# Moving the relation gathers of a graph-and-expert kernel: nine a step in its first pass, the rest behind the expert tiles of block 2

## The chip, the cores and the metric

The kernel runs on one core of a Trainium2 chip. A core has five engines that run their own instruction streams: TensorE (PE: matrix multiplications, with weight loads PEld), VectorE (DVE), ScalarE (ACT), GpSimd (POOL) and SyncE (SP, which here only issues transfers and loads registers). Transfers are made by 16 DMA engines; SP, ACT and POOL each feed them from a queue of their own. Every stream is in order: an instruction that waits holds all that follow it on the same engine. The metric is the device time of one execution in microseconds (us), lower is better.

## What is computed

The reference is a stack of four blocks, each added to its input, over 3125 nodes of 256 values with 103125 edges sorted by destination:

```
x = x + gnn(layernorm(x))         # block 1: 3 layers, mean over in-edges, two 256x256 products
x = x + moe16(layernorm(x))       # block 2: 16 experts, hidden 512, best 2 by gate; layernorm at the end
x = x + clifford(layernorm(x))    # block 3, below
x = x + moe8(layernorm(x))        # block 4: 8 experts, hidden 1024, best 2
```

Block 3 is where the relations come in:

```
h_src = h_hc[src]
r_uv  = r_hc[edge_type]                       # one of 500 relation rows per edge
m = clifford_linear(h_src * r_uv, msg_w, msg_b)
gate = sigmoid(r_uv @ gate_w.T + gate_b)
m = m * gate * norm                           # norm from the degrees of both ends
h_agg = segment_sum(m, dst)
h_out = clifford_linear(h_hc + h_agg, upd_w, upd_b)
```

For each edge the row of its relation has to be fetched from a table of 500 rows (256 values and the gate, 257 floats). The rows do not depend on the nodes, only on the edges' types, so they can be fetched long before block 3 needs them.

## The kernel before

**Blocks and slots.** The nodes lie in NB = 25 blocks of 128. Block 1's first pass over the blocks (L640 to L664, a loop of NB + 3 = 28 steps, software-pipelined over up to four blocks) sorts each destination block's edges into 26 tiles of 128 slots. A step loads a window of edges for block i (`load`, L512, `win`; each half has its place read into a register of SP), ranks them on VectorE (`rank`, L522 `kb`, L531 `member` from TensorE's `prior`, L533, L536), permutes and lays out block i-1 (`permute`, `lay`: TensorE's `ends`, ScalarE's `held` at L587, VectorE's `main_t`, the relation number of every slot), builds adjacency cells for block i-2 (`build`: `oh_end` on VectorE, `block` on TensorE, `cell` on ScalarE, stored by SP at L631) and finishes the first layer for block i-3 (`sums_of` with `z` on TensorE, `finish` on VectorE). Layers 2 and 3 follow as two passes that read the stored cells back; they are called layer 1 and layer 2 in the code, and nothing of them is edited.

**Relation groups.** There are 25 x 26 = 650 slot tiles. Their relation rows are gathered three tiles at a time, 217 groups. `fetch_relations(n, after)` issues the next n groups: VectorE writes the three columns of indices into `paced` (L296) by an operation that also reads `after`, and so it can run only when `after` is there; GpSimd gathers three times 128 rows (L300, an indirect DMA each) into a staging tile `rel_rows` (four buffers); and then `store_relations` has SP write the group before it to DRAM, `r_seq` (L311). Block 3 later reads the groups back in order (`rg_seq`, L1396). So `after` decides when a group is gathered at the earliest. A scheduler puts each engine's instructions in order when the kernel is built, by when their inputs should be there; a group whose `after` is early may so be placed far ahead of where the code has it.

Before the change the groups are fetched so: 95 in pass 1 (up to four a step: one paced by the rank's `qi` at L558, two by `moved` of blocks i-1 and i-2 at L649 and L652, one by `done`, what `finish` returns, at L664), 50 in each of the next two passes, 10 in block 2 after its routing has found the best experts (`top_v`), and the last 12 after block 2's tiles in the code, with `after=beta`. As `beta` is a small load made at the start of block 2, the scheduler puts the 12 ahead of the tiles too.

**Block 2.** `moe` (L922) routes the nodes: it finds the best two experts for each, gives each pair a place, and writes the token indices `tok_g` (L1065), the weights `wt_q` (L1075) and each tile's expert number. Then 34 tiles of 256 tokens run (`expert_tile`, L1119 to L1176): SP loads the expert number into a register and issues the loads of `w1_t` and `w2_t` (L1122, L1125, three buffers each); GpSimd gathers two `xt` of 128 rows two tiles ahead (L249); TensorE transposes them (`pt`, L1130), multiplies (`ph`, L1145), ScalarE and VectorE apply the ReLU (`hid`), TensorE multiplies again (`py`, L1163); VectorE scales (`y`, L1166, eight buffers), and GpSimd scatters with addition into `f_total` (L1168). The two scatters of a tile touch different rows and do not wait for one another, but the first of a tile waits until those of the tile before have landed. After each tile up to the 34th `moe` calls `beside(t)`, which here adds `beta` to one block of `xs`. A loop for further tiles follows (L1188), which does not run with these inputs; all engines meet at its test, and their transfers must have landed.

**Block 3.** Its preparation (L1216 to L1297) loads weights (`mw`, `uw`, L1237) and makes the kernels `km` and `ku`, reads `f_total` back, applies the layernorms, and writes for each of the 25 blocks a scaled copy `hs` (four buffers), split into `hc_part` for TensorE and stored by SP to `hc_rows` (L1285). Then the messages: for 650 main tiles TensorE selects the source rows (`hg_ps`, L1422) and VectorE multiplies with `rg_seq` (`prod`, L1425); 225 spill tiles gather source rows `hg` from `hc_rows` and relation rows `rg` with GpSimd (L249) instead.

**Room.** `paced` and the staging tiles live in pools of `rel_ctx` (L283 to L285), which is closed after block 2 (L1204). The pools that block 3 opens next take that room, and their tiles wait until its last readers and writers are done.

Of the kernel before, what the change touches and what calls it, by code (L numbers as in the profile page):

```python
# [37 lines left out]
F32 = mybir.dt.float32  # L38
BF = mybir.dt.bfloat16
F16 = mybir.dt.float16  # L40
I32 = mybir.dt.int32
# [7 lines left out]
P = 128  # L49
N = 3125  # L50
NB = 25
# [28 lines left out]
def gnn_moe_kernel(  # L80
# [166 lines left out]
    def gather(pool, table, width, ids, name, bufs):  # L247
        rows = pool.tile([P, width], F32, name=name, bufs=bufs)
        nc.gpsimd.indirect_dma_start(out=rows, out_offset=None, in_=table,  # L249
                                     in_offset=bass.IndirectOffsetOnAxis(ap=ids, axis=0))  # L250
        return rows
# [70 lines left out]
    with ExitStack() as block:  # L322
# [66 lines left out]
        with ExitStack() as first:  # L389
# [251 lines left out]
            for i in range(NB + 3):  # L641
                if i < NB:
                    loaded[i] = load(i)
                    ranked[i] = rank(i, loaded[i])
                if 0 <= i - 1 < NB:
                    moved[i - 1] = permute(i - 1, loaded.pop(i - 1), *ranked.pop(i - 1))
                    lay(i - 1, moved[i - 1])
                    if i > 1:
                        fetch_relations(1, words_of(moved[i - 1]))  # L649
                if 0 <= i - 2 < NB:  # L650
                    if i > 2:
                        fetch_relations(1, words_of(moved[i - 2]))  # L652
                    built[i - 2] = build(i - 2, moved.pop(i - 2))
                for b in range(i * SB, min((i + 1) * SB, NB)):
                    spread(b, 0, psum.tile([P, D + 1], F32, name="z", bufs=2)[:, :D],
                           psum.tile([P, 4, P], F32, name="block", bufs=2).rearrange(
                               "p a q -> p (a q)"))
                if i == 3:
                    nc.sync.dma_start(base, x)
                if 0 <= i - 3 < NB:  # L660
                    z = sums_of(i - 3, built.pop(i - 3), 0, psum)
                    done = finish(i - 3, z, 0)
                    if i > 3:
                        fetch_relations(1, done.bitcast(I32))  # L664

        with ExitStack() as flags:
            one = flags.enter_context(tc.tile_pool(name="g0_deg0", bufs=1))
# [252 lines left out]


    def moe(tag, n_exp, hidden, b1, w1, w2, b2, act, ln, x_rows, total, usual,  # L922
            beside=lambda t: None):

# [4 lines left out]
        with ExitStack() as block:  # L931
# [176 lines left out]
            with ExitStack() as run:  # L1108
# [10 lines left out]
                def expert_tile(t):  # L1119
                    e = nc.sync.value_load(exp_i[0:1, t:t + 1], min_val=0, max_val=n_exp - 1)  # L1120
                    w1_t = wpool.tile([P, 1, KD, hidden], F32, name="w1_t")
                    nc.sync.dma_start(w1_t, w1[bass.ds(e, 1), :, :].rearrange(  # L1122
                        "e (p k) f -> p e k f", k=KD))
                    w2_t = wpool.tile([P, 1, nj, D], F32, name="w2_t")
                    nc.sync.dma_start(w2_t, w2[bass.ds(e, 1), :, :].rearrange(  # L1125
                        "e (j p) d -> p e j d", p=P))
                    pt = psum.tile([P, KD, TS], F32, name="pt")
                    for half, xt in enumerate(ahead.pop(t)):
                        for k in range(KD):
                            nc.tensor.transpose(pt[:, k, half * P:(half + 1) * P],  # L1130
                                                xt[:, k:D:KD], ident)
                    xT = work.tile([P, KD, TS], F32, name="xT")
                    for k in range(KD):
                        if ln is None:
                            nc.vector.tensor_copy(xT[:, k, :], pt[:, k, :])  # L1135
                        else:
                            nc.vector.tensor_scalar(xT[:, k, :], pt[:, k, :],
                                                    ln_t[:, 0, k, t:t + 1], ln_t[:, 1, k, t:t + 1],
                                                    op0=ALU.mult, op1=ALU.add)
                    hid = work.tile([P, nj, TS], F32, name="hid")  # L1140
                    for j0 in range(0, nj, 2):
                        ph = psum.tile([P, 2, TS], F32, name="ph", bufs=3)
                        for j in range(j0, j0 + 2):
                            for k in range(KD):
                                nc.tensor.matmul(ph[:, j - j0, :],  # L1145
                                                 w1_t[:, 0, k, j * P:(j + 1) * P], xT[:, k, :],
                                                 start=k == 0, stop=k == KD - 1)
                        for j in range(j0, j0 + 2):
                            if act == AF.Relu and j % 2:
                                nc.vector.tensor_scalar(hid[:, j, :], ph[:, j - j0, :],  # L1150
                                                        b1_t[:, j, t:t + 1], 0.0,
                                                        op0=ALU.add, op1=ALU.max)
                            else:
                                nc.scalar.activation(hid[:, j, :], ph[:, j - j0, :], act,  # L1154
                                                     bias=b1_t[:, j, t:t + 1])
                    for half in range(TS // P):
                        q = t * (TS // P) + half
                        of = slice(half * P, (half + 1) * P)
                        py = psum.tile([P, D], F32, name="py")
                        nc.tensor.matmul(py, oh[:, t:t + 1].to_broadcast([3 * 32, P]), b2_sb,  # L1160
                                         start=True, stop=False)
                        for j in range(nj):
                            nc.tensor.matmul(py, hid[:, j, of], w2_t[:, 0, j, :], start=False,  # L1163
                                             stop=j == nj - 1)
                        y = work.tile([P, D], F32, name="y", bufs=8)
                        nc.vector.tensor_scalar(y, py, wt_q[:, q:q + 1], None, op0=ALU.mult)  # L1166

                        st = nc.gpsimd.indirect_dma_start(  # L1168
                            out=total, in_=y, in_offset=None,
                            out_offset=bass.IndirectOffsetOnAxis(ap=tok_s[:, q:q + 1], axis=0),  # L1170
                            compute_op=ALU.add)
                        if half:
                            tc.declare_no_dep(st.ins, group=f"{tag}_add{t}", reason="other rows")
                        tc.add_to_no_dep_group(f"{tag}_add{t}", st.ins)
                    if t < usual:
                        beside(t)  # L1176

                def run_tiles(first, end):
                    for t in range(first, min(first + 2, end)):
# [15 lines left out]
    with ExitStack() as block:  # L1195
        keep = block.enter_context(tc.tile_pool(name="f0_tokens", bufs=1))
        beta = keep.tile([P, D], F32, name="beta")
        nc.scalar.dma_start(beta, bcast(f0_beta, D))
        fetch_relations(10, top_v[:, NB - 1, :].bitcast(I32))
        moe("f0", 16, 512, f0_b1, f0_w1, f0_w2, f0_b2, AF.Relu, None, f0_x, f0_total, 34,  # L1200
            lambda t: t < NB and nc.vector.tensor_add(xs[:, t, :], xs[:, t, :], beta))
        fetch_relations(len(of_group), beta.bitcast(I32))
        store_relations()
    rel_ctx.close()  # L1204

# [4 lines left out]
    f1_x = dram.tile([NP, D], F32, name="f1_x")  # L1210
    f1_total = dram.tile([NP + TS, D], F32, name="f1_total")
    with ExitStack() as block:
        keep = block.enter_context(tc.tile_pool(name="g1_keep", bufs=1))
        h = keep.tile([P, NB, D], F32, name="hc")

# [104 lines left out]
        with ExitStack() as run:  # L1320
# [80 lines left out]
            def summands():  # L1401


                for b in range(NB):
# [5 lines left out]
                    for n, (_, spilled, t) in enumerate(order):  # L1410
                        ids = spill_d[:, b, :] if spilled else main_d[:, b, :]
                        if t % DG == 0:
                            d_oh[spilled] = drops(ids[:, t:min(t + DG, ids.shape[1])])
                        prod = work.tile([P, W], F32, name="prod", bufs=4)
                        if spilled:
                            hg = gather(work, h_rows, W, spill_s[:, b, t:t + 1], "hg", 6)
                            rg = gather(work, r_rows, W, spill_t[:, b, t:t + 1], "rg", 6)
                        else:
                            sh = t - (t > b)
                            hg = psum.tile([P, W], F32, name="hg_ps", bufs=3)  # L1420
                            for i in (2, 1, 0):
                                nc.tensor.matmul(hg, s_oh[:, t, :], part[:, sh, i, :W],  # L1422
                                                 start=i == 2, stop=i == 0)
                            rg = relation(b * NS + t)
# [76 lines left out]
```

## Time and profile before

| | |
|---|---|
| median of 3 runs | 3060.95 us (3058.07 to 3086.63) |
| profiled execution | 3058.8 us, span 3056.9 us, mean granted TensorE clock 0.914 |
| pass 1 | about 100 to 667 us |
| layers 1 and 2 | 667 to 1323 us |
| block 2: routing, tiles, loop exit | to 1396, 1428 to 1725, 1729.5 us |
| block 3: preparation, messages | 1730 to 1814, 1814 to 2546 us |
| block 4 | 2546 to 3057 us |
| busy over the span | PE 81%, DVE 57%, POOL 51%, ACT 14% |
| relation gathers | 650, 765 us of POOL, mean 1177 ns |

The stages are read off the first and last instructions of their lines. The profile comes from one execution and gives for every group of instructions its line, engine, operation, tiles, count, busy time, mean duration, and what ended the idle time before it; "<-issue" means that nothing the profile shows was waited for. PEclk is the clock that TensorE was granted, as a share of full speed.

### The profile page before, as it was taken

Reading aid. Unit: us, or ns where it says so; the run is one execution under the profiler, and the core shown is the slowest. Engines: PE = TensorE matmul, PEld = TensorE weight load, DVE = VectorE, ACT = ScalarE, POOL = GpSimd, SP = SyncE. Lnnn points to the kernel's source line nnn. Section 1 sums busy time; section 2 is a strip of 40 time slices with the busy share of each in tenths; the row PEclk is TensorE's granted clock in tenths of the full one; section 3 lists DMA queues with packets and bytes.
Section 4 is the critical chain, followed back from the end, with each engine's and each line's share of the span. In section 5 each row is a group of like instructions: output and inputs, shape, how many; then the busy total and the mean of one; then the engine's idle time right before and its main releaser. Section 6 shows DMA issues by size and latency. Waiting matters only on the chain. (4 is left out here: it accounts for less than half of the span.)

```text
span 3056.9 us, 47874 instructions
## 1 busy us (share of the span) xinstructions
PE 2490.5 (81%) x17712; PEld 1978.3 (65%) x17712; DVE 1754.0 (57%) x4664; ACT 432.4 (14%) x1119; POOL 1568.3 (51%) x1383
## 2 busy tenths in 40 slices
PE   1877667769878999943999419999999996899997
PEld 0565556645667588832888306777777775788886
DVE  6978777856555466651333377888788887111110
ACT  1311211213000300000111050000000000222221
POOL 1176876761455166675566326666666660333331
PEclk9988888879989999966999759999999997899998
DMA  5156665663667278865888447777777771766663
GB/s 181 38 176 183 178 188 169 180 211 98 214 199 233 94 253 277 258 183 162 223 200 200 95 148 247 252 248 247 244 245 245 250 217 31 225 181 180 180 176 94
DMA packets 294159, 581.10 MB, mean 190 GB/s; under 512 B 77947, under 2 KB 176956, under 8 KB 289940
## 3 DMA queue, kind: packets, MB, share of 16 engines
q1 hardware_dynamic: 204243, 386.35, 37.2%
q0 software_dynamic: 76992, 177.86, 23.4%
q10 hardware_dynamic: 12672, 13.65, 1.5%
q8 instruction: 145, 2.38, 0.3%
q14 instruction: 107, 0.87, 0.1%
HBM read 433.05 MB, written 151.13 MB: 191 GB/s over the span
## 5 line engine op out<-in xcount | busy, mean ns | idle before, releaser
L300 POOL DMA_INDIRECT rel_rows<-r_rows,paced x650 | 765.1, 1177 | 657.4 <-issue 158.2
L363 PE MATMUL z<-part_hi,cell 128*128 128x256 bf16 x3750 | 685.7, 284 | 27.2 <-issue 26.2
L360 PE MATMUL z<-part_lo,cell 128*128 128x256 bf16 (+1 forms) x1875 | 531.8, 284 | 23.9 <-issue 19.2
L1434 PE MATMUL ps<-prod,d_oh 128*128 128x257 f32 x1750 | 519.7, 391 | 28.9 <-issue 15.1
L363 PEld LDWEIGHTS <-cell 128*128 128x128 bf16 x3750 | 373.3, 101 | 96.7 <-issue 43.4
L1422 PE MATMUL hg_ps<-hc_part,s_oh 128*128 128x257 bf16 x1950 | 328.4, 275 | 106.4 <-DMA hg<-hc_rows,spill_s 106.4
L1168 POOL DMA_INDIRECT f_total<-y,tok_s x126 | 198.3, 1574 | 351.9 <-DVE y L1166 277.0
L249 POOL DMA_INDIRECT hg<-hc_rows,spill_s x225 | 234.0, 1040 | 266.3 <-DVE prod L1425 128.6
L1163 PE MATMUL py<-w_t,hid 128*128 128x256 f32 x1472 | 335.1, 382 | 8.6 <-ACT hid L1154 8.6
L1145 PE MATMUL ph<-xT,w_t 128*128 128x256 f32 x1472 | 335.5, 385 | 0.8
L1425 DVE TENSOR_TENSOR prod<-hg_ps,rg_seq 128x257 f32<-128x257 f32 x650 | 270.0, 421 | 103.9 <-PE hg_ps L1422 67.9
L1434 PEld LDWEIGHTS ps<-prod,d_oh 128*128 128x128 f32 x1750 | 276.1, 191 | 81.1 <-issue 31.3
L1422 PEld LDWEIGHTS <-s_oh 128*128 128x128 bf16 x1950 | 191.5, 99 | 204.0 <-DVE s_oh L1378 106.8
L1166 DVE TENSOR_SCALAR y<-py,wt_q 128x256 f32<-128x256 f32 x126 | 60.9, 484 | 444.9 <-PE py L1163 433.4
L1163 PEld LDWEIGHTS py<-w_t,hid 128*128 128x128 f32 x1472 | 273.9, 191 | 55.8 <-ACT hid L1154 9.0
L1145 PEld LDWEIGHTS ph<-xT,w_t 128*128 128x128 f32 x1472 | 279.8, 192 | 43.7 <-DVE xT L1135 3.1
L249 POOL DMA_INDIRECT rg<-r_rows,spill_t x225 | 234.3, 1041 | 68.6 <-issue 68.6
L360 PEld LDWEIGHTS <-cell 128*128 128x128 bf16 x1875 | 191.7, 102 | 54.8 <-issue 24.7
L1154 ACT ACTIVATE hid<-ph,b_t 128x256 f32<-128x256 f32 x300 | 129.4, 471 | 650.0 <-PE ph L1145 621.8
L249 POOL DMA_INDIRECT xt<-f_x,tok_g x126 | 123.5, 980 | 94.1 <-DVE wt_q L1075 38.3
L501 DVE TENSOR_TENSOR oh_end<-held,iota 128x1024 bf16<-128x1024 f16 (+3 forms) x150 | 150.2, 1016 | 0.2
L862 DVE TENSOR_REDUCE some_src<-cell 128x25 f32<-128x3200 bf16 x25 | 87.2, 3487 | 93.8 <-DMA cell<-cells 79.5
(307 smaller groups left out, 2821.9 us busy)
## 6 DMA issues: line engine op xcount, KB each, us to landing
r_seq<-rel_rows SPq DMA_DIRECT2D x216, 385.5 KB
rg_seq<-r_seq SPq DMA_DIRECT2D x216, 385.5 KB
w_t<-in_L_ffn_W_dram SPq DMA_DIRECT2D x58, 1024.0 KB
cell<-cells SPq DMA_DIRECT2D x50, 800.0 KB
w_t<-in_L_ffn_w_dram SPq DMA_DIRECT2D x68, 512.0 KB
s_row<-main_s SPq DMA_DIRECT2D x25, 832.0 KB
cells<-cell SPq DMA_DIRECT2D x25, 800.0 KB
rel_rows<-r_rows,paced POOLq DMA_INDIRECT x650
```

Source lines behind the costliest of these rows:

```text
L249: nc.gpsimd.indirect_dma_start(out=rows, out_offset=None, in_=table, in_offset=bass.IndirectOffsetOnAxis(ap=ids, axis=0))
L300: nc.gpsimd.indirect_dma_start(out=rows[:, j, :], out_offset=None, in_=r_rows, in_offset=bass.IndirectOffsetOnAxis(ap=types[:, j:j + 1], a ...
L360: nc.tensor.matmul(z[:, :width], cell[:, sh, :], part_lo[:, sh, :width], start=sh == 0, stop=False)
L363: nc.tensor.matmul(z[:, :D], cell[:, sh, :], part_hi[:, sh, i, :], start=False, stop=sh == NB - 1 and i == 1)
L501: nc.vector.tensor_tensor(oh[:, :n, :, :], ids[:, :, None, :].to_broadcast([P, n, width, 2]), table[:, None, :width, :].to_broadcast([P, n ...
L1145: nc.tensor.matmul(ph[:, j - j0, :], w1_t[:, 0, k, j * P:(j + 1) * P], xT[:, k, :], start=k == 0, stop=k == KD - 1)
L1154: nc.scalar.activation(hid[:, j, :], ph[:, j - j0, :], act, bias=b1_t[:, j, t:t + 1])
L1163: nc.tensor.matmul(py, hid[:, j, of], w2_t[:, 0, j, :], start=False, stop=j == nj - 1)
L1168: st = nc.gpsimd.indirect_dma_start(out=total, in_=y, in_offset=None, out_offset=bass.IndirectOffsetOnAxis(ap=tok_s[:, q:q + 1], axis=0), ...
L1422: nc.tensor.matmul(hg, s_oh[:, t, :], part[:, sh, i, :W], start=i == 2, stop=i == 0)
L1425: nc.vector.tensor_mul(prod, hg, rg)
L1434: nc.tensor.matmul(ps[b], d_oh, prod, start=is_first, stop=is_last)
```

## The change

It edits four places. Pass 1 loses the group that `finish` paced: 24 groups, so nine gathers a step at most in place of twelve. `moe` hands each tile's last `y` to `beside`. In block 2 thirteen groups instead of ten are fetched behind `top_v`; after tiles 2, 5, ... 32 one group is fetched with `after=y`, and after the last tile (t = 33) all that are left. The last are 22: 71 in pass 1, 100 in the two layers, 13 and 11 make 195 of 217. And block 3 opens a pool `late` before its others, with `prod`, `hg` and `rg` in it, with the same numbers of buffers as before (4, 6, 6), so that it is these that lie in the room of `rel_ctx`.

```diff
                 if 0 <= i - 3 < NB:
                     z = sums_of(i - 3, built.pop(i - 3), 0, psum)
-                    done = finish(i - 3, z, 0)
-                    if i > 3:
-                        fetch_relations(1, done.bitcast(I32))
+                    finish(i - 3, z, 0)
...
-            beside=lambda t: None):
+            beside=lambda t, y: None):
...
                     if t < usual:
-                        beside(t)
+                        beside(t, y)
...
-        fetch_relations(10, top_v[:, NB - 1, :].bitcast(I32))
-        moe("f0", 16, 512, f0_b1, f0_w1, f0_w2, f0_b2, AF.Relu, None, f0_x, f0_total, 34,
-            lambda t: t < NB and nc.vector.tensor_add(xs[:, t, :], xs[:, t, :], beta))
-        fetch_relations(len(of_group), beta.bitcast(I32))
+
+        def beside(t, y):
+
+            if t < NB:
+                nc.vector.tensor_add(xs[:, t, :], xs[:, t, :], beta)
+            fetch_relations(len(of_group) if t == USUAL - 1 else t % 3 == 2, y.bitcast(I32))
+
+        USUAL = 34
+        fetch_relations(13, top_v[:, NB - 1, :].bitcast(I32))
+        moe("f0", 16, 512, f0_b1, f0_w1, f0_w2, f0_b2, AF.Relu, None, f0_x, f0_total, USUAL,
+            beside)
         store_relations()
     rel_ctx.close()
...
     with ExitStack() as block:
+
+        late = block.enter_context(tc.tile_pool(name="g1_late", bufs=4))
         keep = block.enter_context(tc.tile_pool(name="g1_keep", bufs=1))
...
-                        prod = work.tile([P, W], F32, name="prod", bufs=4)
+                        prod = late.tile([P, W], F32, name="prod")
                         if spilled:
-                            hg = gather(work, h_rows, W, spill_s[:, b, t:t + 1], "hg", 6)
-                            rg = gather(work, r_rows, W, spill_t[:, b, t:t + 1], "rg", 6)
+                            hg = gather(late, h_rows, W, spill_s[:, b, t:t + 1], "hg", 6)
+                            rg = gather(late, r_rows, W, spill_t[:, b, t:t + 1], "rg", 6)
```

In the order of instructions that the build gives the changed kernel, GpSimd has 45 relation gathers ahead of the first token gathers of block 2 (59 before), three more after every third tile between the first scatter of a tile and the next token gathers, ten before the loop's test, and 61 behind it. SP has the loads of `mw` and `uw` ahead of block 2's tiles (before: behind them), 11 relation stores between the tiles' weight loads, and after the loop 12 relation stores, then the other ten mixed with the first seven stores of `hc_rows`; the other 18 of `hc_rows` stand behind the last relation store.

## The prediction

> **What bounds the kernel now.** The chain of waits gives TensorE 37% of the span, spread over stages with different limits, so I read windows, stage by stage. The columns are busy time of TensorE, its weight loads, VectorE, ScalarE and GpSimd, then granted clock, DMA share and GB/s.
>
> ```profile
> 131.00:661.00 530.00, 388.31 (x4731) 308.69 (x4729) 410.21 (x912) 111.63 (x279) 373.43 (x278) 0.86 0.59 178
> 1450.00:1700.00 250.00, 247.37 (x1197) 209.42 (x1197) 82.42 (x189) 29.75 (x63) 155.74 (x122) 0.99 0.80 201
> 1730.00:1760.00 30.00, 0.00 (x0) 0.00 (x0) 18.50 (x88) 1.91 (x4) 0.00 (x0) 0.50 0.41 112
> 1760.00:1814.00 54.00, 0.00 (x0) 0.00 (x0) 45.82 (x186) 40.81 (x108) 0.00 (x0) 0.50 0.21 73
> ```
>
> Row 1 is pass 1, 24 steps of 530/24 = 22.1 us: VectorE is busy 77%, no engine full. Row 2, the tiles of block 2, is TensorE's (99%). Rows 3 and 4 are the preparation of block 3: TensorE and GpSimd idle. Next, in pass 1, one group (count | busy, mean ns | idle before):
>
> ```profile
> L300 POOL DMA_INDIRECT rel_rows<-r_rows,paced x278 | 374.9, 1349 | 156.9 <-issue 72.5 <-DVE paced L296 29.9 <-DVE main L599 20.7
> ```
>
> Each gather also costs 0.30 us between two, so twelve take 12 x 1.65 = 19.8 of a step's 22.1 us. Nothing in pass 1 reads the rows; only SP waits for them, and loads queue behind it. The waits of 131 to 661 us (total us, times, longest):
>
> ```profile
> SPq L311 <- DMA rel_rows<-r_rows,paced: 164.5, 50, 6.7
> ...
> DVE kb L522 <- DMA win<-edge_words: 24.1, 7, 9.3
> DVE free L597 <- ACT held L587: 23.2, 9, 7.3
> DVE member L531 <- PE prior L528: 23.1, 9, 11.2
> DVE member L531 <- remote: 16.2, 4, 6.8
> DVE kb L522 <- issue: 8.8, 2, 5.0
> ```
>
> VectorE idles 530 - 410 = 120 us; 33 of them are waits for the window load, which SP issues behind relation stores. The others are latencies of TensorE and ScalarE. Then the seam into block 2's tiles, waits first (1397 to 1450 us), then GpSimd's and SP's timelines (start, us):
>
> ```profile
> PE pt L1130 <- DMA xt<-f_x,tok_g: 32.6, 3, 30.6
> ...
> POOL rel_rows L300 <- DMA r_seq<-rel_rows: 14.2, 2, 13.9
> ```
> ```profile
> 1388.39 0.95 POOL L300 DMA_INDIRECT rel_rows<-r_rows,paced  x1 [0.30 <-issue]
> 1403.25 0.95 POOL L300 DMA_INDIRECT rel_rows<-r_rows,paced  x1 [13.91 <-DMA r_seq<-rel_rows]
> ...
> 1420.74 0.95 POOL L249 DMA_INDIRECT xt<-f_x,tok_g  x1 [0.30 <-issue]
> ```
> ```profile
> 1399.80 17.50 SPq L311 DMA_DIRECT2D r_seq<-rel_rows  x7
> 1417.64 0.36 SPq L1122 DMA_DIRECT2D w_t<-in_L_ffn_w_dram  x1
> ```
>
> tok_g is written at 1396.3, but the token gathers stand behind 59 relation gathers and start at 1420.74; the first weights wait for seven stores until 1417.64. Last, SP before Clifford:
>
> ```profile
> 1762.48 48.29 SPq L1285 DMA_DIRECT2D hc_rows<-hs  x25
> ```
>
> 25 stores in 48.29 us, 1.93 each. Clifford's first gather from hc_rows (1814.00) needs all of them, and TensorE sits 106.4 us until it.
>
> **Part 1, pass 1: nine gathers a step.** 24 groups leave: 72 gathers, 24 stores, 24 paced writes. Now 9 x 1.65 = 14.9 us of 22.1, and SP is held less. Gone: 24 x 0.15 = 3.6 us of VectorE, and the 33 us of window waits (8 steps). What is late next is the wait for prior: eight steps without a window wait show about 2.5 us there, 8 x 2.5 = 20 comes back. So 3.6 + 33 - 20 = 17 us. Bounds: nothing, if the window is late for other reasons; 50 us, if a good third of the 120 idle us goes. A loss is excluded: nothing is added here. I take -17, nearest to the waits' own row.
>
> VectorE's own operations should not get shorter: put takes 0.668 to 0.696 us in all 66 executions, while the gather goes from 0.94 to 6.46 us, so here it is the gather that waits. The Trainium skill (SBUF — State Buffer, "Who interferes with whom") says that VectorE and GpSimd share a port pair which whoever issues first holds for a whole instruction while the other blocks. If VectorE were the blocked one, 72 gathers fewer could by that free it for up to 72 x 0.95 = 68 us; the constant 0.69 us speaks against it, and I count zero.
>
> **Part 2, the start of block 2's tiles.** 45 relation gathers now precede the token gathers (as before until 1388.4), the other 14 do not. Tokens can start at 1396.5, 24 us earlier. SP, after its last store (gather 45 lands some 3 us after 1389.3), still runs 26 register loads of expert numbers at 0.56 us (30 of them filled the gap before 1399.80): 1393 + 14.6 = 1407.6, so weights go out 10 us earlier and, with 8.0 us to land as before (1417.64 to 1425.6), are there at 1415.6. The same seam in block 4, where no relations stand in the way, takes 16 us from token indices to the first ph: 1396.5 + 16 = 1412.6. First ph was at 1432.17, so -17 to -20; I take -18. The 8.6 us that the first py waited for hid has no cause I can name; it may stay.
>
> The four Clifford weight loads now issue on SP ahead of the tiles (3.62 + 3.29 us at 1731.5): hidden behind the routing until 1396; uncovered they cost 7.
>
> **Part 3, gathers inside the tiles.** 11 groups, one per three tiles, 3 x 1.25 = 3.75 us each on GpSimd. Its groups between 1450 and 1700:
>
> ```profile
> L1168 POOL DMA_INDIRECT f_total<-y,tok_s x60 | 94.8, 1580 | 77.3 <-DVE hid L1150 29.7 <-DVE y L1166 21.1 <-issue 20.7
> L249 POOL DMA_INDIRECT xt<-f_x,tok_g x57 | 56.3, 988 | 18.7 <-issue 11.3 <-PE pt L1130 3.5 <-PE py L1163 2.4
> ```
>
> Three tiles take TensorE 23.5 us and GpSimd 6 x 1.58 + 6 x 0.99 + 12 x 0.30 = 19.0, leaving 4.5 for 3.75. But a pair of scatters waits for the last pair's landing: without gathers pairs stand 6.3 us apart (1717.19 to 1723.46), 2.9 of it that wait. The two token gathers (2.6) fill it; three more make it 6.3, so 18.8 + 3.4 = 22.2 of 23.5. GpSimd keeps up by a hair. Queued behind each relation gather are the next tokens and scatters, and behind its store on SP the weights three tiles ahead; the writes of VectorE follow y in its own order and wait for nothing new. A group moves 395 KB twice: by the page's queues (23.4% of the span for 177.86 MB, 37.2% for 386.35) an estimate of 1.6 + 1.2 = 2.8 us of all DMA engines, so their share goes from 0.80 to about 0.92. The fall behind can be 0 to 15 us at the end; I take 4. Four gathers of the last batch (5 us) stand before the loop's exit. Exit: -18 + 4 + 5 = -9, range -20 to +2.
>
> **Part 4, what is left over.** 22 groups come at the last tile: 61 gathers run after the exit. GpSimd is idle there (rows 3, 4), so they look free, 61 x 1.25 = 76 of 84.4 us (1729.6 to 1814.0). They aren't, because of SP: in the built order hc_rows stores 8 to 25 stand behind the last relation store, and hs has 4 buffers, so 11 of 25 blocks can be made meanwhile. At 1.30 us a gather, 79 + 3 landing + 14 x 1.93 + 3 to the first gather = 112 us, not 84.4: +28. Bounds: +16 (76 us, 11 blocks left, 21 us), and with pass 1's 1.65 a gather, 101 + 3 + 27 + 3 = 134, +50. The row nearest is 1.25 beside 1.04 + 0.30 for block 3's own gathers, so 1.30.
>
> The room for late: km waited 3.8 us for the weight mw; that goes, but under the 79 us of gathers it is worth zero (up to 10 without them). prod, hg, rg keep their buffer counts. Six spill gathers moved ahead of the slow loop end (8 us) before the stores do.
>
> Sum against the profiled 3058.8 us (span 3056.9 plus 1.9): -17 - 9 + 28 = +2, 3061. The median of the runs is 2 us above the profiled one: 3063.
>
> **Rivals.**
> A, slower: SP holds block 3 longer. With gathers at 1.65 us beside a busy VectorE, part 4 is +50, and if the tiles give the start back (exit 0) and pass 1 gives 5, the net is +45: 3106. It decides when the 61 gathers take more than 1729.6 + 95 or so. For it: 1.35 us means in pass 1. Against: 0.95 in quiet stretches. 0.25.
> B, faster: pass 1 runs at the pace of its queues throughout and saves 50, the exit -15, part 4 +20: -45, 3016. For: steps without a wait take 17.5 us. Against: five pauses of 6 to 11 us there have no relation in them. 0.18.
> C, the change does not do what it says in pass 1: windows stay late, 0 - 9 + 28 = +19, 3080; within 1%.
> The forecast with C: 0.57.
>
> **Numbers.** 1% is 31 us, about what a measurement of this kernel can tell. The bounds together reach from 3059 - 50 - 20 + 16 to 3059 + 52; cutting a tenth at each end gives 3020 to 3103. Faster 0.18, same 0.55, slower 0.27.
>
> **What would show it.** Right: window waits of kb near zero and step near 21.4 us; token gathers at 1396 less pass 1's gain, tile pace 7.83 us; after the exit hc_rows stores spread over 80 us and ending some 112 after it. Wrong: hc_rows ending with the old 84, pass 1 steps under 20.5 us, or TensorE idle between tiles.

## The result, and the profile after

In 20 runs each the changed kernel took 3077.91 us (3063.84 to 3094.63) and the kernel before 3060.49 (3049.26 to 3086.63): a ratio of 1.0046, 95% interval 1.0025 to 1.0066, so slower by some 14 us and inside 1%. The profiled execution took 3094.6 us, 17 above its own median; a second pair of traces (`before_again`, `after_again` below, on another chip) is therefore set beside it, in which the trace of the changed kernel is 13 us below its median. That chip took 3115 us for the kernel before, and the two of the other eight experiments 2943 and 2942: absolute times are compared only within one set.

Where the time went, as the change in each stage's length (us; + is longer):

| stage | by | forecast | result's traces | second pair |
|---|---|---|---|---|
| pass 1 | last `raw_dst` | -17 | -42.8 | -50.6 |
| layers 1, 2, routing | `tok_g` | 0 | +21.9 | +7.7 |
| seam into the tiles | first `y` | -18 | -22.1 | -33.0 |
| tiles, first to last `y` | | +4 | +48.9 | +40.9 |
| last `y` to the loop's exit | `rs_main` | +5 | +2.4 | +3.0 |
| exit to the first `hg` gather | | +28 | +40.8 | +41.6 |
| messages, block 4 | end | 0 | -13.2 | -10.5 |

The forecast's terms add up to +2, the traces' to +36 and -1; the medians say +17 and +11.

Windows of the changed kernel (columns as before): pass 1 in its 490 us, a part of the tiles, and the preparation of block 3 in two parts.

```profile
131.00:621.00 490.00, 375.52 (x4716) 300.94 (x4716) 407.37 (x889) 110.92 (x279) 300.65 (x209) 0.90 0.53 160
...
1600.00:1700.00 100.00, 81.92 (x359) 67.49 (x358) 24.80 (x59) 9.01 (x19) 57.56 (x48) 0.88 0.67 164
1738.00:1768.00 30.00, 0.00 (x0) 0.00 (x0) 27.96 (x111) 7.87 (x18) 20.86 (x21) 0.50 0.84 281
1768.00:1863.00 95.00, 0.00 (x0) 0.00 (x0) 41.52 (x161) 35.76 (x94) 46.00 (x47) 0.50 0.66 167
```

In pass 1 TensorE does the same matmuls in 376 us where it took 388, at a granted clock of 0.90 for 0.86, and VectorE's share rises to 83%. In the tiles TensorE falls from 99% to 82%, and the DMA share does not rise to 0.92 but falls to 0.67: on average the DMA engines have room there. The preparation takes 125 us for 84, and in its second part VectorE and ScalarE are busy less than half the time.

The waits of pass 1 after the change (total us, times, longest):

```profile
DVE kb L522 <- DMA win<-edge_words: 29.8, 5, 10.2
...
DVE member L531 <- PE prior L528: 21.8, 11, 4.8
...
DVE free L597 <- ACT held L587: 2.0, 3, 1.0
```

The window wait is still there: 29.8 us, for 24.1 + 8.8 before. What shrank is the wait for TensorE and for ScalarE: `member` from 23.1 + 16.2 to 21.8, `free` from 23.2 to 2.0.

The seam: GpSimd's first token gather, at once after `wt_q`.

```profile
1376.94 0.94 POOL L249 DMA_INDIRECT xt<-f_x,tok_g  x1 [5.67 <-DVE wt_q L1073]
```

The tiles: waits of TensorE and of SP between 1500 and 1722 us.

```profile
PE pt L1128 <- DMA xt<-f_x,tok_g: 23.8, 6, 6.2
PE ph L1143 <- DMA w_t<-in_L_ffn_w_dram: 8.2, 1, 8.2
```
```profile
SPq L311 <- DMA rel_rows<-r_rows,paced: 93.8, 4, 24.9
```

Until the 15th tile `y` comes every 7.9 us, nearly as before; then every third tile takes 10 to 18.7 us. The first scatter of a tile starts 1 us after the tile's first `y` at first, and 22 to 29 us after it from the 17th tile to the 30th: GpSimd is some three tiles behind. Being behind is not new: in the kernel before the same scatter trails by 14 to 17 us from the fifth tile to the 30th, with TensorE full. TensorE then waits for tokens that stand on GpSimd behind three relation gathers, and SP sits for up to 24.9 us at a relation store, with the weight loads behind it. (In the kernel before, SP had no such wait between 1480 and 1712 us.) Token gathers, which landed 2.7 to 3.2 us after their issue ended, take 3.9 to 5.3 (medians of parts of the stage, from the completion records of GpSimd's queue).

SP behind the loop's exit (1738.3 us):

```profile
1739.69 46.26 SPq L311 DMA_DIRECT2D r_seq<-rel_rows  x12
1786.05 0.41 SPq L1292 DMA_DIRECT2D hc_rows<-hs  x1
...
1828.21 1.44 SPq L311 DMA_DIRECT2D r_seq<-rel_rows  x2
1829.76 29.64 SPq L1292 DMA_DIRECT2D hc_rows<-hs  x18
```

That is the picture that the forecast drew: twelve relation stores, then both kinds mixed, and 18 stores of `hc_rows` after the last relation store. They end at 1859.4, and the first `hg` gather starts at 1863.1. The first and the last of GpSimd's 61 relation gathers there:

```profile
1739.03 0.95 POOL L300 DMA_INDIRECT rel_rows<-r_rows,paced  x1 [5.54 <-PEq L917]
...
1823.22 1.07 POOL L300 DMA_INDIRECT rel_rows<-r_rows,paced  x1 [0.30 <-issue]
```

### The profile page after: what moved, and what is told of

The parts are those of the page before. It is cut to its first block, busy times and chain, and to the rows that moved or that the text cites. A ratio compares the mean times of both kernels' runs of the same rounds, so it can differ in the third digit from the quotient of the medians.

```text
span 3092.9 us, 47848 instructions
## 1 busy us (share of the span) xinstructions
PE 2501.1 (81%) x17712; PEld 1983.2 (64%) x17712; DVE 1758.8 (57%) x4664; ACT 433.1 (14%) x1119; POOL 1566.7 (51%) x1383
## 5 line engine op out<-in xcount | busy, mean ns | idle before, releaser
L363 PE MATMUL z<-part_hi,cell 128*128 128x256 bf16 x3750 | 689.6, 285 | 24.2 <-issue 23.5
L360 PE MATMUL z<-part_lo,cell 128*128 128x256 bf16 (+1 forms) x1875 | 534.0, 285 | 21.8 <-issue 16.8
L1441 PE MATMUL ps<-prod,d_oh 128*128 128x257 f32 x1750 | 515.4, 389 | 21.9 <-DVE prod L1432 12.1
L1143 PE MATMUL ph<-xT,w_t 128*128 128x256 f32 x1472 | 348.7, 395 | 23.7 <-DMA w_t<-in_L_ffn_w_dram 22.0
L1143 PEld LDWEIGHTS ph<-xT,w_t 128*128 128x128 f32 x1472 | 289.5, 199 | 71.0 <-issue 24.6
L1161 PEld LDWEIGHTS py<-w_t,hid 128*128 128x128 f32 x1472 | 272.2, 190 | 50.6 <-issue 4.7
```

Source lines behind the costliest of these rows:

```text
L360: nc.tensor.matmul(z[:, :width], cell[:, sh, :], part_lo[:, sh, :width], start=sh == 0, stop=False)
L363: nc.tensor.matmul(z[:, :D], cell[:, sh, :], part_hi[:, sh, i, :], start=False, stop=sh == NB - 1 and i == 1)
L1143: nc.tensor.matmul(ph[:, j - j0, :], w1_t[:, 0, k, j * P:(j + 1) * P], xT[:, k, :], start=k == 0, stop=k == KD - 1)
L1441: nc.tensor.matmul(ps[b], d_oh, prod, start=is_first, stop=is_last)
```

## Experiments

The theory to be tested had three terms: pass 1 gains some 40 us, the gathers in the tiles cost some 45, the leftovers behind the exit some 40. Four kernels, on one chip; the kernel before took 2942.64 us there. Here and below a ratio is to the kernel before on the same chip, with its 95% interval; the us beside it are the difference of the medians, and the two can differ by up to 6 us.

**`p1_back`: pass 1 as before.** Nine groups are left for the tiles, none for the end.

```diff
-                    finish(i - 3, z, 0)
+                    done = finish(i - 3, z, 0)
+                    if i > 3:
+                        fetch_relations(1, done.bitcast(I32))
```

> The changed kernel with pass 1 as before (twelve gathers a step); so 9 groups go into block 2's tiles and none is left behind them. Theory (three terms: pass 1 gains some 40 us, gathers in the tiles cost some 45, the 61 gathers behind the loop some 40): pass 1 ends near 668 us again, the loss in the tiles is somewhat smaller (9 groups for 11: 25 to 40 us between first and last y beyond the 264 us of before), the preparation takes 84 us again, and the whole is within 10 us of the kernel before. Rival (pass 1's gain is taken back by the layers anyway, half of it was gone by the routing in the first profile): the whole is 20 us or more below the kernel before, as it then loses only half of the gain and saves the 40 behind the loop.

Measured: 1.0055 (1.0036 to 1.0074), +22 us. Pass 1 ends at 638.9 us, against 602 to 605 in the three kernels beside it with nine gathers: 35 us. On this chip nearly all of that is the window wait, here and in `hc_act` (VectorE's waits from 158 us to the end of pass 1):

```profile
DVE kb L522 <- DMA win<-edge_words: 73.4, 18, 9.6
```
```profile
DVE kb L522 <- DMA win<-edge_words: 40.3, 16, 10.0
```

The layers and the routing after it take no share back: 685 us in both. The tiles take 308.1 us from first to last `y` against 260.1 in the kernels without gathers there: nine groups cost 48, more than expected. From the exit to `hg` 76.1 us: with nothing left over, and the weights of `km` loaded early, 8 less than the kernel before. The rival (20 us below) falls; the theory missed its bound of 10 us by 12 (by 6, if the ratio is taken), on the price of the tiles.

**`hc_act`: the stores of `hc_rows` from ScalarE.**

```diff
-                    nc.sync.dma_start(h_rows[b * P:(b + 1) * P, :], hs)
+                    nc.scalar.dma_start(h_rows[b * P:(b + 1) * P, :], hs)
```

> The changed kernel with the 25 stores of hc_rows issued by ScalarE in place of SP, so that they do not stand behind the relation stores. Theory (SP's order holds them): from the loop's exit to the first hg gather 95 us (61 gathers of 1.25 us and some pauses are 85, six spill gathers 8) in place of 125, the whole 25 to 30 us below the changed kernel. Rival (the gathers themselves, or ScalarE's 1.9 us a block, hold block 3): 115 us or more, the whole within 10 us of the changed kernel.

Measured: 1.0151 (1.0125 to 1.0178), +49 us, and 118.7 us from exit to `hg`. The theory fails as it was put. ScalarE's waits in that stage say why:

```profile
ACT hc_part L1293 <- DMA r_seq<-rel_rows: 37.0, 7, 9.4
```

ScalarE, which now issues these stores, waited seven times for relation transfers on SP. The semaphores in this trace show how: the 22 relation stores of SP and the 25 stores of ScalarE count their completions on the same eight semaphores, and each of the seven waits ends when a relation store completes on the semaphore that the next store of `hc_rows` will use (the first at 1703.10 us, and that store is issued at 1703.19). So moving the stores to another engine's queue did not part the two kinds. This run alone could not tell that hold from GpSimd's own work; `tail_no_store` does.

**`none_in_tiles`: all 33 groups after the last tile.**

```diff
-            fetch_relations(len(of_group) if t == USUAL - 1 else t % 3 == 2, y.bitcast(I32))
+            fetch_relations(len(of_group) if t == USUAL - 1 else 0, y.bitcast(I32))
```

> The changed kernel with no relation groups after tiles 2, 5, ... 32: all 33 left are fetched after the last tile. Theory: the tiles run at 7.83 us again, last y 40 to 50 us earlier, and the stage from the exit to the first hg grows by 11 x 3 x 1.25 = 41 us to some 165; the whole within 10 us of the changed kernel. Rival for the tiles (they slow down by the weights or the clock, not by the gathers in them): the tiles stay slow and the whole is 40 us above the changed kernel.

Measured: 1.0060 (1.0040 to 1.0081), +24 us. First to last `y` 260.1 us; in `hc_act`, whose tiles are those of the changed kernel, 316.4. The gathers in the tiles cost 56 us on this chip, and the rival (slow tiles without them) falls. From the exit to `hg` 149.0 us, where the theory had 165.

**`p1_to_l1`: the kernel before, with its 24 groups moved from pass 1 to layer 1.**

```diff
-                    done = finish(i - 3, z, 0)
-                    if i > 3:
-                        fetch_relations(1, done.bitcast(I32))
+                    finish(i - 3, z, 0)
...
-                fetch_relations(1, done.bitcast(I32))
+                fetch_relations(2 if b else 1, done.bitcast(I32))
```

> The kernel before with one edit: the 24 groups that finish paced in pass 1 are fetched in layer 1 (two after each of its blocks but the first); block 2 and block 3 as before. Theory: pass 1 ends some 40 us earlier and layer 1, where GpSimd is busy 43% and nothing waits for the rows, takes back 0 to 15; the whole 25 to 40 us below the kernel before. Rival (layers take the gain back): within 10 us of the kernel before.

Measured: 1.0053 (1.0034 to 1.0072), +16 us: the rival, and worse. Pass 1 ends at 604.7 as hoped, but from there to the first step of layer 2 it takes 450 us, against 408 in `none_in_tiles` with 24 groups fewer in layer 1. VectorE waits 162 us there for the cells that SP loads, for 122, and SP 284 us for relation rows, for 251. So here too a group has a price, by the loads of SP that stand behind its store; a stage in which GpSimd is half idle is not free.

Four more, on the chip that took 3115.21 us for the kernel before.

**`before_again` and `after_again`: both kernels unchanged.**

> The kernel before, unchanged, for a trace from the chip of these runs. The chip of the first four runs took 2943 us for it where the one of the result took 3060. Both theories: pass 1 ends some 36 us later than in the changed kernel, tiles at 7.83 us, first hg gather 84 us after the loop's exit.

> The changed kernel, unchanged, beside it. Theory (pass 1 pays some 36, the start of the tiles some 20 more; the gathers in the tiles cost about 50 and the leftovers behind the exit about 40): the sum is +25 to +40 us on the kernel before, with first to last y some 315 us and 120 to 125 us from the exit to the first hg gather. Rival (the ratio of the result, 1.0046, holds on any chip): +14.

Measured: `after_again` 3126.6 us, 1.0029 (0.9991 to 1.0067). The interval holds both "no change" and the result's 1.0046; the +25 to +40 of the theory is out (+25 would be 1.008). The table above has the stages: the leftovers cost 42 as the theory had it, but pass 1 paid 51 and the start of the tiles 33, more than it had allowed, and the gathers in the tiles cost 41, less than its 50.

**`tail9`: pass 1 as before, no gathers in the tiles, the nine left after the last tile.**

```diff
+                    done = finish(i - 3, z, 0)
+                    if i > 3:
+                        fetch_relations(1, done.bitcast(I32))
...
-            fetch_relations(len(of_group) if t == USUAL - 1 else t % 3 == 2, y.bitcast(I32))
+            if t == USUAL - 1:
+                fetch_relations(len(of_group), y.bitcast(I32))
```

> Pass 1 as before (twelve gathers a step), 13 groups ahead of the tiles, none in the tiles, and the 9 that are left after the last tile; late as in the changed kernel. Theory: tiles at 7.83 us and started 20 us or more earlier than in the kernel before, as fewer gathers stand before the tokens; the 27 gathers behind the exit (34 us) fit under the 76 us that the preparation took with none. 15 to 30 us faster than the kernel before. Rival (whatever is queued behind the exit is paid in full): 9 x 3.75 = 34 us on the preparation, so no faster than the kernel before.

Measured: 3077.23 us, 0.9883 (0.9833 to 0.9932): 38 us faster than the kernel before, and the interval lies below that of `after_again` too. Its tiles (window of the trace), and SP behind the exit at 1711.4 us:

```profile
1440.00:1690.00 250.00, 249.37 (x1215) 211.46 (x1215) 83.89 (x192) 30.35 (x64) 157.30 (x121) 1.00 0.79 192
```
```profile
1714.59 33.92 SPq L311 DMA_DIRECT2D r_seq<-rel_rows  x9
1748.61 48.78 SPq L1295 DMA_DIRECT2D hc_rows<-hs  x25
```

TensorE is full in the tiles, and they start 38 us earlier than in `before_again`. All 25 stores of `hc_rows` stand behind nine relation stores, but 34 us is little more than the 32 that the preparation needed before its first such store in the kernel before (1730.0 to 1762.5): 89.5 us to `hg`, for 84.1. Neither free nor paid in full (34).

**`no_store`: the groups in the tiles gathered, not stored there.**

```diff
+            if stored:
+                landing.append((i, rows))
...
+        last, rows = landing[-1]
+        for i in range(last + 1, last + 12):
+            nc.sync.dma_start(r_seq[i], rows.rearrange("p r w -> p (r w)"))
```

> The changed kernel with the 11 groups in the tiles gathered but not stored from there; their places in r_seq are filled ahead of the tiles with rows of another group, so the output is not the reference's. It tells what in the tiles costs 50 us. Theory (the weights of the tiles are held on SP behind stores that wait for late gathers): first to last y falls to 280 us or less. Rival (GpSimd's own queue is too long with 3.75 us more in one landing gap of three): it stays above 300.

Measured, in a single run: first to last `y` 283.0 us; `after_again` 308.8, `tail9` 260.1, on the same chip. Between the two lines that were drawn: of 49 us the stores hold 26 and the gathers alone cost 23. Without the stores SP waits for no relation row in the tiles, and tokens land in 2.4 to 3.3 us (medians) again; the scatters trail by up to 19 us, little more than the 14 to 17 of the kernel before, whose tiles run at full pace. How the gathers alone slow the tiles is therefore not shown: TensorE is idle for 23 of 250 us in this run, and of the waits that the profile names for it (14 us) only 2.3 are for tokens.

The last four, on a chip with 2942.16 us for the kernel before.

**`one_a_tile` and `spread9`: one gather after each tile**, in the changed kernel, and with pass 1 as before (nine groups, none left over).

```diff
+            for j, t in enumerate(g):
+                after = yield
...
-            fetch_relations(len(of_group) if t == USUAL - 1 else t % 3 == 2, y.bitcast(I32))
+            if t < USUAL - 1:
+                parts.send(y.bitcast(I32))
```

> The changed kernel with the same 33 gathers in the tiles, one after each tile (a group is complete after three) in place of three after every third; all else as changed. Theory (three gathers in one landing gap are too long for GpSimd's queue, one fits: 2.57 + 1.25 us against a gap of 2.9): first to last y falls from about 310 to 285 us or less, the whole 20 us or more below the changed kernel's +0.3 to 0.5%. Rival (the stores on SP ahead of the weights cost it, wherever the gathers stand): above 300 us.

> Pass 1 as before (twelve gathers a step), and the 9 groups that are then left gathered one gather a tile; none behind the exit. If one gather a tile is nearly free (first to last y 270 us or less): 25 us or more below the kernel before, like tail9 or better. If not (285 us): about 10 us below it.

Measured: `one_a_tile` 1.0090 (1.0056 to 1.0123), first to last `y` 288.7 us; `spread9` 0.9997 (0.9974 to 1.0020), 286.4 us. `tail_no_store` below ran on this chip and has the gathers and stores of the changed kernel in its tiles: 308.6 us. Against it spreading takes back 20 us of the 48 above 260 (the tiles without gathers on the two other chips), between the lines of 285 and 300. SP still waits for relation rows (192 us in twelve waits, 206 in eleven there), and TensorE for weights (18 us, 35 there). The whole of `one_a_tile` (+25 us) is not the 20 below the changed kernel that was expected of it, but the changed kernel did not run on this chip. `spread9` came out as its "if not" branch says, though equal to the kernel before and not 10 us below. Its pass 1, with twelve gathers, ends at 620.8 us, where `one_a_tile` and `tail_no_store` with nine end at 600.8 and 603.8: on this chip the gain of pass 1 is 17 to 20 us, and it is again the window wait (59.8 us, against 42.1 and 39.4).

**`gathers_only`: three unread gathers a step put back into pass 1.** In `finish`'s place the newest group is gathered a second time and not stored, which lets VectorE write that group's indices again.

```diff
-                    finish(i - 3, z, 0)
+                    done = finish(i - 3, z, 0)
+                    if i > 3:
+                        gather_again(done.bitcast(I32))
```

> The changed kernel with three gathers a step put back into pass 1 that nobody reads: at the place of the removed group the newest group is gathered a second time and not stored. It tells whether gathers or stores make pass 1 long. If the gathers on GpSimd and their traffic: pass 1 is 35 to 50 us longer than in the changed kernel, as before. If the stores on SP, with the window loads behind them (what the forecast priced): within 15 us of the changed kernel.

Measured: pass 1 ends at 728.3 us, 125 later than with nine gathers. VectorE's waits:

```profile
DVE paced L310 <- DMA rel_rows<-r_rows,paced: 148.2, 22, 9.5
```

The rewritten columns of `paced` wait for the gathers that still read them, 22 times. The experiment made a wait of its own and decides nothing.

**`tail_no_store`: the 22 leftover groups gathered, not stored there.** The edit is that of `no_store`, for the groups of the last tile.

> The changed kernel with the 22 leftover groups gathered behind the last tile but not stored there; their places in r_seq are filled ahead of the tiles with rows of another group, so the output is not the reference's. GpSimd's work behind the exit is the same, and no store stands before or shares a queue with those of hc_rows. Theory (the stores of hc_rows are held by the relation stores): from exit to the first hg gather 84 to 100 us in place of 125. Rival (the 61 gathers slow the preparation in another way): above 110 us.

Measured: 98.7 us from the exit (1680.9) to `hg`. SP, then GpSimd:

```profile
1705.77 54.99 SPq L1298 DMA_DIRECT2D hc_rows<-hs  x25
```
```profile
1761.81 0.94 POOL L300 DMA_INDIRECT rel_rows<-r_rows,paced  x1 [0.30 <-issue]
1768.84 0.94 POOL L249 DMA_INDIRECT rg<-r_rows,spill_t  x1 [6.09 <-issue]
...
1779.56 1.38 POOL L249 DMA_INDIRECT hg<-hc_rows,spill_s  x1 [3.54 <-issue]
```

The stores of `hc_rows` run through by 1760.8, and now GpSimd's own queue sets the start: 61 gathers until 1762.8, six spill gathers, then `hg`. `one_a_tile`, on the same chip and with the stores, took 125.8. `spread9`, on this chip too and with nothing left over, took 76.2. So of 50 us the stores make 27, and GpSimd's queue 23, with two pauses in it (6.1 us before `rg`, 3.5 before `hg`) for which the profile names no wait.

## Why the prediction was right, and where it was not

The time lay in the range and within 1%, 15 us above 3063 and 2 below rival C's 3080, but not for the reasons of either: two large terms, pass 1 and the tiles, were mis-sized by 26 to 45 us each, with opposite signs, and cancelled. That the sum came out close is luck. Two of the prediction's three signs of being wrong were there: steps of 490/24 = 20.4 us in pass 1, and TensorE idle between tiles. (Its bounds reach from 3005 to 3111; a tenth off each end makes 3016 to 3100 and not 3020 to 3103. The result lies in both.)

**Part 1** failed at "3.6 + 33 - 20 = 17". It priced one wait, the window's. In the result's traces the window waits stayed (29.8 us of 32.9), and in the second pair they grew from 17 to 40. What shrank there is the wait of `member`, which reads TensorE's `prior`: in the second pair it fell from 73 to 11 us. Before, then after (for "remote" the profile names no engine):

```profile
DVE member L531 <- remote: 63.0, 10, 10.0
...
DVE member L531 <- PE prior L528: 10.1, 7, 1.9
```
```profile
DVE member L531 <- PE prior L528: 6.9, 4, 3.7
...
DVE member L531 <- remote: 3.8, 2, 2.6
```

TensorE's busy time for the same some 4520 matmuls fell from 374 to 346 us there, at a clock of 0.91 for 0.85 (367 to 353 in the result's traces). On the two faster chips `member` waits for 2.4 us at most, with nine gathers or twelve, and the window waits do shrink, by 28 to 33 us where the gain is 34 to 37, and by 17 to 20 where it is 17 to 20: what Part 1 described happened there, on the last chip even in its size. So the gain is shown in all four sets (43, 51, 34 to 37 and 17 to 20 us), and which wait gives it differs with the chip. A step is a loop through three engines and a load, and the wait that a change removes in one trace need not be the one it removes in the next; that is how I read it. What makes TensorE's clock rise, and whether the gathers or their stores lengthened the step, is open, as `gathers_only` failed; the window waits on the faster chips point to SP's queue. Rival B had this gain (50), but neither its tiles nor its tail. Of the five pauses that it counted against itself as none of the relations' doing, most come and go between runs of one kernel: TensorE, VectorE and ScalarE idle for over 3 us together in pass 1 six times in the first trace of before, once in the second.

VectorE was rightly left at zero: its busy time went from 385.2 to 382.0 us, the 24 index writes, and `put` stayed at 0.67 to 0.72 us. The rule of the Trainium skill (SBUF — State Buffer, "Who interferes with whom") has the later of VectorE and GpSimd block, for VectorE's instructions that use the shared ports; here it is GpSimd's gather that got longer, from 1.35 to 1.44 us on average, as VectorE's share rose. No run here shows that this lock is the reason.

**Part 2** had the mechanism right, and its sum by two errors: tokens at once after `tok_g`, first `ph` 22.6 us after it for 35.8, so -13 for -18, and 9 us more from the unnamed wait for `hid`, which went too; first `y` -22. The first weights went out 19 us after `tok_g` and not 11: the 26 register loads of SP took 20.0 us, not 14.6, as 0.56 us is the step of the undisturbed ones alone (30 had taken 22.4 us in the kernel before).

**Part 3** failed at "GpSimd keeps up by a hair". 22.2 of 23.5 us counted undisturbed landings, and left out that the scatters already trail `y` by 14 to 17 us in the kernel before. The queue fell further behind, and late gathers held SP's stores, with the weights behind them, while tokens landed later. +41 to +56 us, where 15 was the bound; a little under half by the gathers alone (`no_store`), the rest by their stores on SP.

**Part 4** had the mechanism right, and the sign; +41 lay inside its +16 to +50. Mis-sized were the gathers (79 us, measured 85.3, with pauses of 2.3 and 4.6 us), the landing of the last group (3 us, measured 5.4 to the end of its store) and the blocks left (14 x 1.93 = 27, measured 18 stores in 29.6). That its `hc_rows` stores stand "behind the last relation store" is 27 us of it (`tail_no_store`).

Not foreseen, and left open: the unedited layers and routing took 22 and 8 us longer. On the two faster chips they take as long with twelve gathers in pass 1 (685 and 688 us) as with nine (684 to 691), so nothing there is paid back for pass 1. The messages took 13 and 11 us less; in the second set the three traces with the pool `late` agree (1256.2 to 1256.8 us from `hg` to the end, 1267.3 without it), but on the chip of the first four experiments the messages take 687 to 693 us with it and 688 without, so `late` is not shown to have done that.

## What to carry to other kernels

In this kernel a prefetch had a price at each place where its store shares an in-order queue with loads that something waits for: 24 groups cost 17 to 51 us in pass 1, by the chip, 42 in layer 1, and a group in the tiles 4 to 5, though GpSimd was not full in any of these. Fit a prefetch into idle time only as far as that time lasts before the next critical store (nine groups behind the exit did well, 22 did not), and leave a stage that is full on one engine alone. When an added wait has slack by a sum of averages, ask what happens after it first runs late: whether the lateness dies out or holds the next load as well. And read the waits on more than one chip: here the same gain in pass 1 came out of the wait for the window on two chips, and mostly out of the wait of `member` for TensorE's `prior` on the second pair's.

## What the runs showed of the hardware

Stores issued by ScalarE waited for transfers of SP's queue (37 us in seven waits of `hc_act`), as both counted completions on the same eight semaphores. One unedited kernel took 2942, 2943, 3060 and 3115 us on the four chips of these runs. The mean clock differs by less: 0.923 to 0.929 in its runs on the two fastest, 0.903 to 0.915 on the slowest. So an edit is compared only beside its own runs.
